# Epsilon, power and shift of two layer norms: from VectorE and GpSimd to GpSimd alone, between its softmax divisions

## The chip, the core and the metric

The kernel runs on one core of a Trainium2 chip. The core has a matrix engine (TensorE, PE in the profile; its weight loads are shown as PEld), a vector engine (VectorE, DVE), an activation engine (ScalarE, ACT), a general engine (GpSimd, POOL) and a sync engine that only issues transfers here (SyncE, SP). Each runs its own list of instructions in the order in which they were written, and waits for the others by semaphores. The metric is the device time of one execution in microseconds; before the change the median of three runs is 1526.4 us (1526.15 to 1528.2).

## The reference

One block of a cross-attention network in float32: 128 sequences of 128 tokens with 256 features, a context of the same size, 16 heads, a hidden layer of 1024. Cut to its core:

```python
q, k, v = heads(query @ Wq + bq), heads(key @ Wk + bk), heads(values @ Wv + bv)
scores = einsum('bhqd,bhkd->bhqk', q, k) / sqrt(16)
attn = softmax(where(j < i, scores, -1e30)); attn[:, :, 0, :] = 0
x = layer_norm(query + (attn @ v) @ Wo + bo, ln1_g, ln1_b)
ffn = relu(x @ W1 + b1) @ W2 + b2
out = layer_norm(x + ffn, ln2_g, ln2_b)

def layer_norm(x, g, b):
    mu = mean(x); var = mean((x - mu) ** 2)
    return (x - mu) * rsqrt(var + 1e-5) * g + b
```

## The kernel before, in words

The sequences are taken in 64 pairs, numbered p. A pair's tokens lie on 128 partitions, so that a tile of a pair has two columns of every per-token number. The work on a pair is spread over several steps of a software pipeline: step(p), which runs for p from 7 to 63, computes scores and softmax of pair p, the attention output and the first norm of pair p - 2, the first layer of the feed-forward part of pair p - 3, its second layer of pair p - 4, and the second norm of pair p - 5. In the steps from 7 to 62 the statistics of the two norms, two columns each, are made together in tiles of four columns; step 63 and the pairs at both ends make them apart.

The order of every engine is written out by hand: no scheduler moves an instruction. What is called first in step() stands first in the list of its engine.

The four-column tiles are mv (mean and variance of four token columns, made by both_stats: bn_stats and bn_aggr, L566 and L569), sd (first variance plus epsilon, L572 on VectorE; then, to the power of -0.5 in place, L1441 on GpSimd) and nb (minus mean times sd, L576 on VectorE, in both_shifts). ScalarE applies a norm as sd times x plus nb: L597 for the first norm (norm1), L634 for the second (norm2).

Around them stand, on GpSimd, the divisions of the softmax (sums, L440): the upper halves of the query rows come in two parts, heads 0 to 7 and heads 8 to 15, the lower halves in one part. In second_by_seven TensorE makes the second layer from seven products of eight matmuls each (L842), a Strassen-like scheme, that add up in three places of PSUM: px, py and pz. After a product, sum_of_seven (L878 on VectorE) adds the place's content to the residual t2; the next product onto the same place may start only when that has been read. In the order of the program: px, py, pz; sum 0 reads px; px again; sum 1 reads py; pz's second half; sum 2 reads px; py again; sums 3 and 4 read pz and py; px again; sum 5 reads px. Between the sums, second_by_seven calls what step() hands it for a given part: transposes of the next tokens (tokens, L250), of the weights that were divided (turn, L459), a reciprocal (L451), and, ahead of sum 5, both_shifts.

Behind that, hidden_by_seven makes the first layer from seven products too (L934, tiles phs); ScalarE and VectorE take part (L944, L947 to L962), and norm1 and norm2 run on ScalarE between them. On GpSimd follow add_bo (L257), residual1 (L609, L612) and finish (L640, L641, gain and bias of the second norm), and in the next step combine_hidden (tile hS, L827 to L830) and combine_normed (tile xS, L896 to L899), ahead of the next divisions.

Of the kernel before, what the change touches and what calls it, by code (L numbers as in the profile page):

```python
# [8 lines left out]
F32 = mybir.dt.float32  # L9
AF = mybir.ActivationFunctionType  # L10
ALU = mybir.AluOpType
AX = mybir.AxisListType

P = 128
NEG_INF = -1e30
LN_EPS = 1e-5
# [3 lines left out]
def tile_cross_attention_block(  # L20
# [22 lines left out]
    nc = tc.nc  # L43
# [19 lines left out]
    const = ctx.enter_context(tc.tile_pool(name="const", bufs=1))  # L63
# [73 lines left out]
    nc.sync.dma_start(c_first[:, 2:4], c[2:4].rearrange("b p d -> p b d"))  # L137
    power = const.tile([P, 4, 1], F32, tag="power", name="power")
    nc.gpsimd.memset(power, -0.5)
    ident = const.tile([P, P], F32, tag="ident", name="ident")  # L140
    make_identity(nc, ident)

# [111 lines left out]
    def add_bo(p):  # L254
        st = states[p]
        st["xb"] = proj.tile([P, 2, D], F32, tag="xb", name=f"xb_{p}")
        nc.gpsimd.tensor_tensor(  # L257
            st["xb"], tokens_of[p // 2][:, p % 2 * 2 : p % 2 * 2 + 2], bov_r[:, None, :].to_broadcast([P, 2, D]), ALU.add
        )
# [110 lines left out]
    def scores_both(p):  # L370

        st = states[p]
        for hi in range(2):
            st["sps", hi] = [
                at_bank(r if hi else (6, 7, 4, 5)[r], f"pss{hi}_{p}_{r}") for r in range(NS)
            ]
            room(p, hi)
        one, two = (0, 1), (2, 3)
        for strips, hi, m in (
            (two, 0, 0), (one, 1, 0), (two, 0, 1), (one, 1, 1),  # L380
            (two, 1, 0), (two, 1, 1), (one, 0, 0), (one, 0, 1),
        ):
            n = P if hi else HP
            for s in range(2):
                for r in strips:
                    strip, first = slice(32 * r, 32 * r + 32), s * P
                    nc.tensor.matmul(  # L387
                        st["sps", hi][r][
                            s * HP : (s + 1) * HP, m * 2 * n : (m + 1) * 2 * n
                        ].rearrange("p (e j) -> p e j", e=2),  # L390
                        st["qT"][strip, m, first + hi * HP : first + hi * HP + HP],
                        st["kT"][strip, m, :, first : first + n],
                        start=True, stop=True,
                    )
# [52 lines left out]
    def reciprocal(p, hi, part):  # L447
        st = states[p]
        rs = small.tile([P, H], F32, tag=f"rs{hi}", name=f"rs{hi}_{p}_{part.start}")
        rs = st["rs", hi, part.start] = rs[:, part]  # L450
        nc.vector.reciprocal(rs, st["su", hi][:, part])  # L451
# [44 lines left out]
    def weigh(p):  # L496

        st = states[p]
        pT = st.pop("pT")
        pc = at_bank(7, f"pc_{p}") if p > 1 else bank(f"pc_{p}")  # L500

        for m in range(KC):
            for s in range(2):
                at = (m * 2 + s) * P
                for j in range(NS):
                    nc.tensor.matmul(  # L506
                        pc[32 * j : 32 * j + 32, at : at + HP],
                        st["vd"][:, s, 4 * m + j].rearrange("p e d -> p (e d)"),
                        pT[:, 2 * s : 2 * s + 2, H + 2 * j + m, :],
                        start=True, stop=True,  # L510
                    )
            for s in range(2):
                at = (m * 2 + s) * P
                for e in range(2):
                    for j in range(NS):
                        nc.tensor.matmul(  # L516
                            pc[32 * j : 32 * j + 32, at + HP : at + P],
                            st["vz"][:, s, 4 * m + j, 2 * e : 2 * e + 2, :].rearrange(
                                "p e d -> p (e d)"
                            ),  # L520
                            pT[:, 2 * s : 2 * s + 2, 4 * j + 2 * m + e, :],
                            start=(e == 0), stop=(e == 1),
                        )
        st["pc"] = pc

    def context(p):
        pc = states[p].pop("pc").rearrange("p (u i) -> p u i", i=P)
        nc.scalar.copy(cxT.rearrange("p m s i -> p (m s) i")[:, :, 1:], pc[:, :, 1:])  # L528
# [29 lines left out]
    def both_stats(p):  # L558

        st, old = states[p - 2], states[p - 5]  # L560
        mv = small.tile([P, 4, 2], F32, tag="mv", name=f"mv_{p}")
        sd = small.tile([P, 4, 1], F32, tag="sd", name=f"sd_{p}")
        nb = small.tile([P, 4, 1], F32, tag="nb", name=f"nb_{p}")
        bs = small.tile([P, 4, 6], F32, tag="bsb", name=f"bsb_{p}")
        for u, t in enumerate((old["t2"][:, 0], old["t2"][:, 1], st["t1"][:, 0], st["t1"][:, 1])):
            nc.vector.bn_stats(bs[:, u], t)  # L566
        reciprocal(p, 1, TWO)
        for u in range(4):
            nc.vector.bn_aggr(mv[:, u], bs[:, u])  # L569
        for s, i, u in ((old, 2, 0), (st, 1, 2)):  # L570
            s["mv", i], s["sd", i], s["nb", i] = (v[:, u : u + 2] for v in (mv, sd, nb))
        nc.vector.tensor_scalar(sd, mv[:, :, 1:2], LN_EPS, None, ALU.add)  # L572
        return mv, sd, nb

    def both_shifts(mv, sd, nb):
        nc.vector.scalar_tensor_tensor(nb, mv[:, :, 0:1], -1.0, sd, ALU.mult, ALU.mult)  # L576

    def attention_sum(p):
        st = states[p]
# [213 lines left out]
    def low_maximum(p):  # L793
        st = states[p]
        nc.vector.tensor_reduce(st["nmx", 0], st["sm", 0], AX.X, ALU.max, negate=True)
# [581 lines left out]
    def step(p):  # L1377
        last = p == NP - 1
        weigh(p - 2)
        context(p - 2)  # L1380
        if p > 7:
            states[p - 4]["rest"].relu(1)
            states[p - 4]["rest"].relu(7)
            states[p - 4]["rest"].relu(3)
            states[p - 4]["rest"].relu(5)
        scores_both(p)
        if last:
            combine_hidden(p - 4, POOL_ALONE)
            add_bo(p - 1)
        else:  # L1390
            combine_hidden(p - 4, POOL_ALONE)
            combine_normed(p - 3)
        if not last:
            load_ahead(p)
        mask(p, 0, B)
        if last:
            mask(p, 0, A)
        mask_high(p, A)
        exponential_by_head(p, 1, ONES, True)
        mask_high(p, B)  # L1400
        exponential_by_head(p, 1, TWOS, True)
        if not last:
            mask(p, 0, A)
        low_maximum(p)
        if not last:
            exponential_by_head(p, 0, range(H), True)
            queries(p + 1)
        attention_out(p - 2)
        if not last:
            reciprocal(p, 1, ONE)  # L1410
        attention_sum(p - 2)
        if last:
            stats(p - 2, states[p - 2]["t1"], 1)
            deviation(p - 2, 1)
            shift(p - 2, 1)
            values(p)
            values_out(p)
            stats(p - 5, states[p - 5]["t2"], 2)
            deviation(p - 5, 2)
            norm1(p - 2)  # L1420
            exponential_by_head(p, 0, range(H), True)
            sums(p, 1, ONE)
            sums(p, 1, TWO)
            shift(p - 5, 2)
            turn_x1(p - 2)
            turn(p, 1, 0)
            second_by_seven(p - 4)
            residual1(p - 3)
            sums(p, 0, ALL)
            turn(p, 1, 1)  # L1430
            hidden(p - 3, range(FC))
            turn(p, 0, 0)
            bring(p, nc.sync, LATE_FIRST[: len(EVERY) // 2])
            return
        project_keys(p + 1)
        copy_keys(p + 1, (0,))
        values(p)
        joint = both_stats(p)
        sums(p, 1, ONE)
        sums(p, 1, TWO)  # L1440
        nc.gpsimd.tensor_tensor(joint[1], joint[1], power, ALU.pow)  # L1441
        ahead = p + 2 < NP
        second_by_seven(p - 4, {
            1: lambda: (tokens(p + 2, "x") if ahead else None, turn(p, 1, 0)),
            2: lambda: tokens(p + 2, "c") if ahead else None,
            3: lambda: (reciprocal(p, 0, ALL), turn(p, 1, 1)),
            5: lambda: both_shifts(*joint),
        })
        sums(p, 0, ALL)
        add_bo(p - 1)  # L1450
        residual1(p - 3)
        hidden_by_seven(p)
        finish(p - 5)
        store(p - 5)
        bring(p, nc.sync, LATE_FIRST)
# [56 lines left out]
    for s in range(2):  # L1512
# [8 lines left out]
        mv = small.tile([P, 2], F32, tag="mvl", name=f"mv_last_{s}")  # L1521
        nc.vector.bn_stats(bs, t2[:, s])
        nc.vector.bn_aggr(mv, bs)
        sd = small.tile([P, 1], F32, tag="sdl", name=f"sd_last_{s}")
# [39 lines left out]
```

## Time and profile before

| | |
|---|---|
| median of three runs | 1526.4 us |
| profiled execution, its own time | 1528.55 us |
| its span, first to last instruction | 1526.8 us |
| mean granted TensorE clock | 0.997 |
| share of the chain that ended last: TensorE | 92% |
| DVE, issue, ACT, POOL, DMA in that chain | 3%, 1%, 1%, 1%, 1% |
| L440, divisions on GpSimd | 192 of 1900 ns, 362.0 us |
| costliest lines of the chain | L934 23%, L842 pX 11%, py 7%, pz 7% |

The profile lists, per engine, how long it was busy, and for each line of the kernel the number of instructions, the mean time of one and what the engine had waited for. The chain is followed back from the last instruction, at each step to what released it; an engine with a large share of it sets the time. In a view by time a row gives start, duration, engine, line, operation and tiles, with x8 for eight such instructions in a row. Durations of neighbouring instructions of one engine overlap a little, since they are pipelined; the distance from start to start is the safer number.

### The profile page before, as it was taken

How to read it: one execution, taken by the hardware profiler on the slowest of the kernel's cores; microseconds unless marked ns; L12 is line 12 of the kernel's file. 1: busy time of each engine (PE TensorE's matmuls, PEld its weight loads, DVE VectorE, ACT ScalarE, POOL GpSimd, SP SyncE). 2: the span in 40 equal slices, each digit the busy share in tenths (PEclk: the TensorE clock that was granted, in tenths of full speed). 3: DMA queues.
4: the chain of work that ended last, by engine and by line, in shares of the span. 5: the costliest groups of instructions: out<-in, count | busy, mean ns of one | idle time of the engine just before them, and what ended most of it. 6: DMA issues, size and time to landing. Idle time of an engine off the chain costs nothing.

```text
span 1526.8 us, 53815 instructions
## 1 busy us (share of the span) xinstructions
PE 1500.5 (98%) x19270; PEld 1387.0 (91%) x19270; DVE 1368.1 (90%) x2835; ACT 1313.8 (86%) x5271; POOL 1258.1 (82%) x1118
## 2 busy tenths in 40 slices
PE   8999999999999999999999999999999999999888
PEld 6788999999999999999999999999999999999887
DVE  7989999999999999999999999999999999999844
ACT  5667999999999999999999999999989999999942
POOL 6878888888888888888888888888888888888862
PEclk9999999999999999999999999999999999999999
DMA  9356655655655565665556656566556556555431
GB/s 199 80 119 144 143 143 135 134 144 125 156 136 131 139 141 133 150 141 133 139 137 138 148 136 139 133 136 141 145 135 135 143 129 152 139 128 132 112 98 42
DMA packets 415318, 204.63 MB, mean 134 GB/s; under 512 B 282448, under 2 KB 383056, under 8 KB 415056
## 3 DMA queue, kind: packets, MB, share of 16 engines
q1 hardware_dynamic: 412768, 199.34, 56.3%
q8 instruction: 158, 2.59, 0.8%
q10 hardware_dynamic: 2288, 1.85, 0.5%
q14 instruction: 104, 0.85, 0.2%
HBM read 70.26 MB, written 33.29 MB: 68 GB/s over the span
## 4 chain that ended last, share of the span: by engine, by line
PE 92%; DVE 3%; ACT 1%; issue 1%; POOL 1%; DMA 1%; SPq 0%; POOLq 0%; DVEq 0%; ACTq 0%
PE phs L934 23%; PE pX L842 11%; PE pq L264 7%; PE py L842 7%; PE pz L842 7%; PE po L535 7%; PE pv L304 7%; PE pk L264 7%; PE pss L387 6%; PE pc L516 3%; PE ph L742 3%; PE pc L506 2%; ACT hT L750 1%; ACT sm L805 0%; PE py L762 0%
## 5 line engine op out<-in xcount | busy, mean ns | idle before, releaser
L440 POOL TENSOR_TENSOR sm<-sm,rs 128x1024 f32<-128x1024 f32 x192 | 362.0, 1900 | 24.8 <-DVE rs L451 18.8
L805 ACT ACTIVATE sm<-pss,nmx 128x128 f32<-128x128 f32 x944 | 328.5, 403 | 40.8 <-issue 36.3
L805 ACT ACTIVATE sm<-sm,nmx 128x64 f32<-128x64 f32 x944 | 313.7, 403 | 0.0
L805 ACT ACTIVATION_READ_ACCUMULATOR sm<-sm,nmx 128x1 f32 x912 | 234.0, 257 | 0.0
L459 DVE STREAM_TRANSPOSE tb<-sm 128x1024 f32<-128x1024 f32 x186 | 223.5, 1204 | 3.3 <-POOL sm L440 3.3
L805 ACT ACTIVATION_READ_ACCUMULATOR sm<-pss,nmx 128x1 f32 x912 | 221.9, 243 | 0.0
L965 ACT ACTIVATE hT<-hT,b1e_c 128x256 f32<-128x256 f32 x448 | 191.1, 499 | 19.2 <-DVE hT L956 19.1
L934 PE MATMUL phs<-xS,w1t 128*128 128x128 f32 x1344 | 159.2, 275 | 0.0
L934 PEld LDWEIGHTS phs<-xS,w1t 128*128 128x128 f32 x1344 | 154.6, 192 | 0.0
L788 DVE TENSOR_REDUCE nmx<-pss 128x4 f32<-128x512 f32 x236 | 151.0, 682 | 0.0
L640 POOL TENSOR_TENSOR t<-t,g_r 128x512 f32<-128x512 f32 x62 | 80.2, 1294 | 84.1 <-ACT t L634 83.9
L827 POOL TENSOR_TENSOR hS<-hT 128x512 f32<-128x512 f32 x57 | 72.3, 1268 | 87.5 <-ACT hT L965 86.4
L842 PE MATMUL pX<-wt,hS 128*128 128x128 f32 x960 | 131.9, 281 | 9.5 <-DVE t L878 5.5
L842 PEld LDWEIGHTS pX<-wt,hS 128*128 128x128 f32 x960 | 117.3, 193 | 18.7 <-issue 17.0
L294 ACT ACTIVATE kT<-pk,bkh,half 128x256 f32<-128x256 f32 x252 | 130.6, 588 | 4.0 <-PE pk L264 4.0
L264 PE MATMUL pq<-xT,wq 128*128 128x256 f32 x504 | 125.4, 392 | 0.0
L535 PE MATMUL po<-wo,cxT 128*128 128x256 f32 x512 | 121.3, 380 | 0.8 <-ACT cxT L528 0.8
L304 PE MATMUL pv<-wv,cT 128*128 128x256 f32 x512 | 121.0, 379 | 0.0
L264 PE MATMUL pk<-cT,wk 128*128 128x256 f32 x504 | 119.2, 379 | 0.0
L934 PE MATMUL phs<-x1T,w 128*128 128x128 f32 x896 | 118.3, 275 | 0.0
L401 DVE TENSOR_TENSOR sm<-pss,neg 128x256 f32<-128x256 f32 (+1 forms) x276 | 108.4, 436 | 6.0 <-PE pss L387 2.5
L535 PEld LDWEIGHTS po<-wo,cxT 128*128 128x128 f32 x512 | 96.9, 190 | 14.5 <-ACT cxT L528 1.3
(170 smaller groups left out, 4046.4 us busy)
## 6 DMA issues: line engine op xcount, KB each, us to landing
pT<-tb SPq DMA_DIRECT2D x976, 96.0 KB, 2.2
x1t<-tbx SPq DMA_DIRECT2D x252, 64.0 KB, 2.7
x1T<-x1t SPq DMA_DIRECT2D x63, 256.0 KB, 3.0
out_dram<-t SPq DMA_DIRECT2D x63, 256.0 KB, 3.2
xb<-in_x_dram SPq DMA_DIRECT2D x124, 128.0 KB, 4.1
cb<-in_ctx_dram SPq DMA_DIRECT2D x124, 128.0 KB, 3.8
x<-in_x_dram SPq DMA_DIRECT2D x31, 512.0 KB, 4.7
w<-in_L_xattn_W_dram SPq DMA_DIRECT2D x2, 1024.0 KB, 8.4
```

The source lines that it names most:

```text
L264: nc.tensor.matmul(ps[:, m * TP : (m + 1) * TP], w[:, k, m * P : (m + 1) * P], src[:, k, :], start=(k == 0), stop=(k == KC - 1),)
L294: nc.scalar.activation(st["kT"][:, m, e, :], pk[:, m * TP : (m + 1) * TP], AF.Identity, bias=bkh[:, m, e : e + 1], scale=half[:, e : e + 1],)
L304: nc.tensor.matmul(pv[:, s * D : (s + 1) * D], st["cT"][:, k, s * P : (s + 1) * P], wv[:, k, :], start=(k == 0), stop=(k == KC - 1),)
L401: nc.vector.tensor_tensor(st["sm", hi][:, 4 * r : 4 * r + 4, :], st["sps", hi][r][:, : 4 * n].rearrange("p (n j) -> p n j", j=n), no[:, No ...
L440: nc.gpsimd.tensor_tensor(sm[:, part, :], sm[:, part, :], rs[:, :, None].to_broadcast([P, part.stop - part.start, n]), ALU.mult,)
L459: nc.vector.transpose(st["tb"][:, :, at : at + 256].rearrange("p j (n a) -> p n j a", a=32), st["sm", hi].rearrange("p h j -> p (h j)")[:, ...
L535: nc.tensor.matmul(po[:, s * D : (s + 1) * D], cxT[:, k, s, :], wo[:, k, :], start=(k == 0), stop=(k == KC - 1),)
L788: nc.vector.tensor_reduce(st["nmx", 1][:, 4 * r : 4 * r + 4], st["sps", 1][r].rearrange("p (n j) -> p n j", j=P), AX.X, ALU.max, negate=True,)
L805: nc.scalar.activation(sm[:, h, :], src, AF.Exp, bias=nmx[:, h : h + 1], scale=1.0, **({"accum_out": st["su", hi][:, h : h + 1]} if summed ...
L842: nc.tensor.matmul(out, left(k), right(k), start=(first and k == 0), stop=(k == FC // 2 - 1), skip_group_check=True,)
L934: nc.tensor.matmul(ps[:, i * P : (i + 1) * P].rearrange("p (n a) -> p n a", a=32), left(i), right, start=(i == 0 and which not in self.ONT ...
L965: nc.scalar.activation(self.hT[:, f], self.hT[:, f], AF.Relu, bias=b1e_c[:, f : f + 1], scale=1.0,)
```

## The change

Two four-column constants are added (epsilon and minus one). The addition of epsilon leaves VectorE's both_stats. both_shifts becomes four tensor_tensor instructions on GpSimd (add epsilon, power, times mean, times minus one), and is called where the power stood before, behind the second of the three divisions; VectorE's call of it ahead of sum 5 goes.

```diff
     power = const.tile([P, 4, 1], F32, tag="power", name="power")
     nc.gpsimd.memset(power, -0.5)
+    eps = const.tile([P, 4, 1], F32, tag="eps", name="eps")
+    nc.gpsimd.memset(eps, LN_EPS)
+    minus = const.tile([P, 4, 1], F32, tag="minus", name="minus")
+    nc.gpsimd.memset(minus, -1.0)
...
-        nc.vector.tensor_scalar(sd, mv[:, :, 1:2], LN_EPS, None, ALU.add)
         return mv, sd, nb

     def both_shifts(mv, sd, nb):
-        nc.vector.scalar_tensor_tensor(nb, mv[:, :, 0:1], -1.0, sd, ALU.mult, ALU.mult)
+        nc.gpsimd.tensor_tensor(sd, mv[:, :, 1:2], eps, ALU.add)
+        nc.gpsimd.tensor_tensor(sd, sd, power, ALU.pow)
+        nc.gpsimd.tensor_tensor(nb, mv[:, :, 0:1], sd, ALU.mult)
+        nc.gpsimd.tensor_tensor(nb, nb, minus, ALU.mult)
...
         joint = both_stats(p)
         sums(p, 1, ONE)
         sums(p, 1, TWO)
-        nc.gpsimd.tensor_tensor(joint[1], joint[1], power, ALU.pow)
+        both_shifts(*joint)
         ahead = p + 2 < NP
         second_by_seven(p - 4, {
             1: lambda: (tokens(p + 2, "x") if ahead else None, turn(p, 1, 0)),
             2: lambda: tokens(p + 2, "c") if ahead else None,
             3: lambda: (reciprocal(p, 0, ALL), turn(p, 1, 1)),
-            5: lambda: both_shifts(*joint),
         })
```

On GpSimd, step 26 as an example, from the last of xS to the residual. Before (a name ends in the number of its buffer; rs_26_0 and rs_26_8 are reciprocals of pair 26):

```order
L899 TENSOR_TENSOR xS_9149<-x1T_9018,xS_9149 128x128
L440 TENSOR_TENSOR sm_9105<-sm_9105,rs_26_0_9219 128x1024
L440 TENSOR_TENSOR sm_9105<-sm_9105,rs_26_8_9244 128x1024
L1441 TENSOR_TENSOR sd_9237<-sd_9237,power 128x4
L440 TENSOR_TENSOR sm_9105<-sm_9105,rs_26_0_9310 128x1024
L257 TENSOR_TENSOR xb_9326<-x_8042,bov_r 128x512
```

The same place after the change, where line numbers are 4 to 6 higher:

```order
L905 TENSOR_TENSOR xS_9172<-x1T_9041,xS_9172 128x128
L444 TENSOR_TENSOR sm_9128<-sm_9128,rs_26_0_9242 128x1024
L444 TENSOR_TENSOR sm_9128<-sm_9128,rs_26_8_9267 128x1024
L579 TENSOR_TENSOR sd_9260<-mv_9259,eps 128x4
L580 TENSOR_TENSOR sd_9260<-sd_9260,power 128x4
L581 TENSOR_TENSOR nb_9261<-mv_9259,sd_9260 128x4
L582 TENSOR_TENSOR nb_9261<-nb_9261,minus 128x4
L444 TENSOR_TENSOR sm_9128<-sm_9128,rs_26_0_9335 128x1024
L261 TENSOR_TENSOR xb_9350<-x_8062,bov_r 128x512
```

Three instructions more stand between the second and the third division; nothing else moves on GpSimd.

On VectorE, the same step, from the statistics to the sum that reads py. Before:

```order
L569 BN_AGGR mv_9236<-bsb_9239 128x2 x4
L572 TENSOR_SCALAR sd_9237<-mv_9236 128x4
L878 TENSOR_TENSOR t_22_8957<-t_22_8957,pX_9256 128x128
L250 STREAM_TRANSPOSE xT_9288<-xb_8410 128x512
L459 STREAM_TRANSPOSE tb_9290<-sm_9105 128x8x4x32
L878 TENSOR_TENSOR t_22_8957<-t_22_8957,py_9257 128x128
```

After:

```order
L573 BN_AGGR mv_9259<-bsb_9262 128x2 x4
L884 TENSOR_TENSOR t_22_8980<-t_22_8980,pX_9281 128x128
L254 STREAM_TRANSPOSE xT_9313<-xb_8431 128x512
L463 STREAM_TRANSPOSE tb_9315<-sm_9128 128x8x4x32
L884 TENSOR_TENSOR t_22_8980<-t_22_8980,py_9282 128x128
```

The sum that reads px now follows the statistics directly; further on in the step, L576 ahead of the last L878 is gone too. Lists of the other engines are the same.

## The prediction

> **What bounds the kernel now.** I read the page's first part, then the instructions that the change touches, then one ordinary step of the steady loop in order of time on each engine (the columns there are start, duration, engine, line, operation, tiles, and in brackets the idle time before it and what ended it).
>
> ```profile
> PE 1500.5 (98%) x19270; PEld 1387.0 (91%) x19270; DVE 1368.1 (90%) x2835; ACT 1313.8 (86%) x5271; POOL 1258.1 (82%) x1118
> L572 DVE TENSOR_SCALAR sd<-mv x56: 282/1586/1818, 155.9 to 1425.1; 128x4 f32<-128x4 f32 x56
> L1441 POOL TENSOR_TENSOR sd<-sd,power x56: 1015/1019/1029, 158.6 to 1428.4; 128x4 f32<-128x4 f32 x56
> L576 DVE SCALAR_TENSOR_TENSOR nb<-mv,sd x56: 459/461/709, 162.0 to 1431.2; 128x4 f32<-128x4 f32 x56
> ```
>
> TensorE (PE) sets the time; what the change is worth is therefore what TensorE waits for in a step. A step lasts (1425.1 - 155.9) / 55 = **23.08 us**. The odd row is L572: adding epsilon to four columns takes 1586 ns on VectorE (DVE), though once it took 282. One ordinary step shows why. TensorE first:
>
> ```profile
> 546.84 1.05 PE L842 MATMUL pX<-w,hT 128*128 128x128 f32 x8
> 547.73 1.06 PE L842 MATMUL py<-wt,hS 128*128 128x128 f32 x8
> 548.62 1.06 PE L842 MATMUL pz<-w,hT 128*128 128x128 f32 x8
> 549.75 1.13 PE L842 MATMUL pX<-wt,hS 128*128 128x128 f32 x8
> 550.72 1.06 PE L842 MATMUL pz<-wt,hT 128*128 128x128 f32 x8
> 551.67 1.13 PE L842 MATMUL py<-w,hS 128*128 128x128 f32 x8
> 552.64 1.06 PE L842 MATMUL pX<-wt,hS 128*128 128x128 f32 x8
> 553.53 0.72 PE L934 MATMUL phs<-x1T,w 128*128 128x128 f32 x5
> ```
>
> These are the seven products of the second layer, eight matmuls each. From start to start an undisturbed one takes 0.89 us (546.84 to 547.73 to 548.62, and 552.64 to 553.53). The fourth product starts 1.13 after the third, that is 0.24 late; it then takes 0.97 instead of 0.89 (0.08 for starting again); the sixth starts 0.06 late and takes 0.08 too long. All seven take 553.53 - 546.84 = 6.69 instead of 7 x 0.8925 = 6.25: **0.44 us of TensorE are lost here in a step.** Now VectorE and GpSimd (POOL) beside it:
>
> ```profile
> 547.47 0.33 DVE L569 BATCH_NORM_AGGREGATE mv<-bsb 128x2 f32<-128x6 f32 x4
> 547.83 1.59 DVE L572 TENSOR_SCALAR sd<-mv 128x4 f32<-128x4 f32 x1
> 549.33 0.27 DVE L878 TENSOR_TENSOR t<-t,pX 128x128 f32<-128x128 f32 x1
> 550.16 1.20 DVE L459 STREAM_TRANSPOSE tb<-sm 128x1024 f32<-128x1024 f32 x1
> 551.28 0.24 DVE L878 TENSOR_TENSOR t<-t,py 128x128 f32<-128x128 f32 x1
> 552.08 0.24 DVE L878 TENSOR_TENSOR t<-t,pX 128x128 f32<-128x128 f32 x1
> ...
> 547.09 0.46 POOL L899 TENSOR_TENSOR xS<-x1T,xS 128x128 f32<-128x128 f32 x1
> 547.50 3.75 POOL L440 TENSOR_TENSOR sm<-sm,rs 128x1024 f32<-128x1024 f32 x2
> 551.21 1.02 POOL L1441 TENSOR_TENSOR sd<-sd,power 128x4 f32<-128x4 f32 x1
> 552.56 1.91 POOL L440 TENSOR_TENSOR sm<-sm,rs 128x1024 f32<-128x1024 f32 x1 [0.33 <-DVE rs L451]
> ```
>
> The fourth product adds onto pX, so it must wait until VectorE has read the first product out of it (L878 t<-t,pX, ends at 549.60; the product starts 0.15 later). The sixth waits in the same way for t<-t,py (ends 551.52, start 0.15 later). Both readers stand behind L572, and L572 ends at 549.42, where the first of GpSimd's two divisions ends (547.50 + 1.90 = 549.40). So the TENSOR_SCALAR does nothing for 1.3 us but wait for a GpSimd instruction to finish. One step of the 56 is a ready-made experiment, because GpSimd came 0.5 us later there:
>
> ```profile
> 1194.34 0.28 DVE L572 TENSOR_SCALAR sd<-mv 128x4 f32<-128x4 f32 x1
> 1196.49 1.25 DVE L459 STREAM_TRANSPOSE tb<-sm 128x1024 f32<-128x1024 f32 x1 [1.05 <-POOL sm L440]
> ...
> 1194.14 0.46 POOL L899 TENSOR_TENSOR xS<-x1T,xS 128x128 f32<-128x128 f32 x1
> ...
> 1195.14 1.06 PE L842 MATMUL pz<-w,hT 128*128 128x128 f32 x8
> 1196.03 1.06 PE L842 MATMUL pX<-wt,hS 128*128 128x128 f32 x8
> 1196.92 1.06 PE L842 MATMUL pz<-wt,hT 128*128 128x128 f32 x8
> 1198.05 1.13 PE L842 MATMUL py<-w,hS 128*128 128x128 f32 x8
> ```
>
> Here L572 waited only for the short L899 (both end at 1194.6) and the fourth product starts 0.89 after the third: **that wait is gone**. But the sixth now starts 0.24 late, since VectorE's transpose L459 waited for the late division. That is the wait that could take its place.
>
> **The change, part by part.**
>
> *L572 goes (56 times).* Without it VectorE, free at 547.80, reads pX as soon as the first product is out, at about 547.9 to 548.2; with the 0.15 seen above the fourth product could start at 548.35, and its undisturbed start is 546.84 + 3 x 0.8925 = 549.52. Cover: 1.2 us. Late next on VectorE is the transpose L459, which needs the first division, at 549.43 instead of 550.16. Everything after it moves 0.73 forward: t<-t,py ends at 550.79, so the sixth product could start at 550.94, against an undisturbed 546.84 + 5 x 0.8925 = 551.30. Cover: 0.36 us. t<-t,pX (552.08 now) ends at 551.6, the seventh product may start at 551.75, undisturbed 552.20: cover 0.44. All 0.44 us lost in a step go. In the first step L572 takes 0.9 and TensorE loses nothing; 55 steps remain: **55 x 0.44 = 24.2 us**.
>
> *L576 goes (56 x 0.46 on VectorE).* It lies ahead of VectorE's own wait for TensorE:
>
> ```profile
> 555.59 0.69 DVE L947 TENSOR_TENSOR hT<-hT,phs 128x512 f32<-128x512 f32 x1 [0.78 <-PE phs L934]
> 554.71 0.59 ACT L944 COPY hT<-phs 128x512 f32<-128x512 f32 x1 [0.94 <-PE phs L934]
> 557.39 1.09 ACT L597 ACTIVATE x<-t,nb,sd 128x256 f32<-128x256 f32 x2
> 559.55 1.29 POOL L640 TENSOR_TENSOR t<-t,g_r 128x512 f32<-128x512 f32 x1 [1.27 <-ACT t L634]
> ```
>
> VectorE idles 0.78 there; the 0.46 only lengthens that idle time. Worth 0. The same rows show the slack when TensorE is 0.44 us earlier: ScalarE (ACT) waits 0.94 for phs and keeps 0.50.
>
> *Three more four-column instructions on GpSimd a step.* The trace has no four-column add or multiply. Nearest rows:
>
> ```profile
> L1198 POOL TENSOR_TENSOR b1e_c<-b1e_c,b_c 128x8 f32<-128x8 f32 x1 | 0.2, 206 | 0.0
> POOL hS L827 <- ACT hT L965: 86.4, 56, 1.6
> POOL t L640 <- ACT t L634: 83.9, 59, 10.3
> POOL sm L440 <- DVE rs L451: 18.8, 55, 1.0
> ```
>
> An add of eight columns takes 206 ns: the lower end. The upper end is the power itself, 1019 ns for four. I take 0.2, since add and multiply are what that row is, and 0.08 before each for the result it reads (L898 ends at 547.01, L899, which reads it, starts at 547.09 in the step above): 3 x 0.28 = 0.84 us, queued between the second and the third division. The third division now waits 0.33 for its reciprocal, so it starts 0.5 later, at 553.1; behind it stand L257, L609, L612 and L640. L640 has 1.27 idle ahead of it, of which 0.44 go to the faster TensorE and 0.5 to this: 0.3 left, and another 1.54 (86.4 / 56) ahead of hS. Cost: **0**. The shift nb comes at about 553.1 instead of 554.5; its reader L597 starts at 557.39. Cost 0. At full price of the upper end the extra is 3.3 us a step, the rival below.
>
> [...]
>
> *Two memsets at the start, 0.1 each*, ahead of the identity that the warm-up reads: 0 to 0.2 us; I take 0.
>
> **Sum.** The profiled execution took 1528.55 us with a span of 1526.8; less 24.2 that is 1504.3. It lies 2.1 above the median of 1526.4; from the median: **1502.2 us**.
>
> **Rivals.**
>
> *The wait moves to the sixth product.* If the first division ended more than 0.36 us later against TensorE than now, the step would become that of 1194: 0.24 + 0.08 lost instead of 0.44, a gain of about 0.13 x 55 = 7 us, so 1519. For: that step exists, and the division follows a chain through a transfer (x1T) and eight GpSimd instructions (hS and xS, four each). Against: that chain starts from phs and is not touched by the change, and it was late in one step of 55; anything between 1502 and 1519 needs a delay between 0.36 and 0.8 in all steps. [...]
>
> *GpSimd becomes the bound (slower).* Its idle time in an ordinary step is 0.33 + 1.27 + 1.54 = 3.14 us. If each small instruction cost as much as the power (1.02 + 0.08, three times 3.3), GpSimd would work through without a pause and the step would be 23.08 + 0.16: 55 x 0.16 = 9 us slower, 1535. It decides at (3.14 / 3) - 0.08 = 0.97 us an instruction. For: the power takes 1.02 with the same four columns. Against: the 206 ns of L1198.
>
> *The waits of TensorE don't hang on L572*, and it stays at 1526: the step at 1194 speaks against it.
>
> **How the numbers follow.** Forecast 0.84 (1499 to 1506: 24.2 by the reading of starts, about 2, and a spread of the runs shown of 2); wait moved, whole or in part, 0.08; no change 0.03; GpSimd bound 0.05. The range of 8 in 10 is the forecast's own, stretched towards a partly moved wait: 1498 to 1511. Faster by over 0.2% (3 us, what a measurement of this kernel can tell): 0.84 + 0.08 = 0.92; same 0.03; slower 0.05.
>
> **What would show it.** Steps of 22.64 us; seven products in 6.25; no issue wait ahead of the fourth; the transpose L459 waiting for GpSimd by about 0.6; small adds and multiplies on GpSimd of 0.2; L640's idle time near 0.3. I would be wrong if the sixth product starts late in every step, if the small instructions take 0.6 or more, or if VectorE shows another long short-tile instruction.

## The result, and the profile after

The changed kernel takes **1504.9 us** (median of four runs, 1504.22 to 1505.53), against 1526.45 us before in the same comparison: a ratio of 0.9856, 95% interval 0.9839 to 0.9874, or 21.5 us. The forecast was 1502.2 us in a range of 1498 to 1511; its gain of 24.2 us corresponds to a ratio of 0.9841, inside the interval.

| | before | after |
|---|---|---|
| profiled execution, its own time | 1528.55 us | 1505.16 us |
| its span | 1526.8 us | 1503.4 us |
| busy: TensorE, VectorE, GpSimd | 1500.5, 1368.1, 1258.1 us | 1482.7, 1275.2, 1288.3 us |

From the page and from the views of the four-column tiles of the kernel after (behind the count: shortest, median and longest duration in ns, first and last start):

```profile
PE 1482.7 (99%) x19270; PEld 1380.9 (92%) x19270; DVE 1275.2 (85%) x2723; ACT 1312.1 (87%) x5271; POOL 1288.3 (86%) x1288
L579 POOL TENSOR_TENSOR sd<-mv,eps x56: 193/203/209, 158.1 to 1404.3; 128x4 f32<-128x4 f32 x56
L580 POOL TENSOR_TENSOR sd<-sd,power x56: 1017/1017/1023, 158.4 to 1404.6; 128x4 f32<-128x4 f32 x56
L581 POOL TENSOR_TENSOR nb<-mv,sd x56: 201/202/203, 159.5 to 1405.7; 128x4 f32<-128x4 f32 x56
```

VectorE is busy 93 us less and GpSimd 30 us more. Neither number is the gain; the gain is in TensorE's order of time. An ordinary step after the change, on TensorE, VectorE and GpSimd:

```profile
1105.68 1.05 PE L848 MATMUL pX<-w,hT 128*128 128x128 f32 x8
1106.57 1.06 PE L848 MATMUL py<-wt,hS 128*128 128x128 f32 x8
1107.47 1.06 PE L848 MATMUL pz<-w,hT 128*128 128x128 f32 x8
1108.36 1.06 PE L848 MATMUL pX<-wt,hS 128*128 128x128 f32 x8
1109.25 1.06 PE L848 MATMUL pz<-wt,hT 128*128 128x128 f32 x8
1110.15 1.06 PE L848 MATMUL py<-w,hS 128*128 128x128 f32 x8
1111.04 1.06 PE L848 MATMUL pX<-wt,hS 128*128 128x128 f32 x8
1111.93 1.06 PE L940 MATMUL phs<-x1T,w 128*128 128x128 f32 x8
...
1107.19 0.29 DVE L884 TENSOR_TENSOR t<-t,pX 128x128 f32<-128x128 f32 x1 [0.56 <-PE pX L848]
1108.27 1.25 DVE L463 STREAM_TRANSPOSE tb<-sm 128x1024 f32<-128x1024 f32 x1 [0.16 <-POOL sm L444]
1109.43 0.25 DVE L884 TENSOR_TENSOR t<-t,py 128x128 f32<-128x128 f32 x1
...
1106.33 3.75 POOL L444 TENSOR_TENSOR sm<-sm,rs 128x1024 f32<-128x1024 f32 x2
1110.04 0.20 POOL L579 TENSOR_TENSOR sd<-mv,eps 128x4 f32<-128x4 f32 x1
1111.85 1.90 POOL L444 TENSOR_TENSOR sm<-sm,rs 128x1024 f32<-128x1024 f32 x1
1117.94 1.29 POOL L646 TENSOR_TENSOR t<-t,g_r 128x512 f32<-128x512 f32 x1 [0.36 <-ACT t L640]
1122.15 1.27 POOL L833 TENSOR_TENSOR hS<-hT 128x512 f32<-128x512 f32 x1 [1.55 <-ACT hT L971]
```

The seven products follow one another at 0.89 us, 1111.93 - 1105.68 = 6.25 in all. The reader of px now waits for TensorE (0.56) and no longer the other way round. The step's length comes from two starts of the first product that lie 54 steps apart, after and before:

```profile
177.65 0.72 PE L848 MATMUL pX<-w,hT 128*128 128x128 f32 x5
1399.94 0.83 PE L848 MATMUL pX<-w,hT 128*128 128x128 f32 x6
```

```profile
177.54 1.05 PE L842 MATMUL pX<-w,hT 128*128 128x128 f32 x8
1423.99 1.05 PE L842 MATMUL pX<-w,hT 128*128 128x128 f32 x8
```

After: (1399.94 - 177.65) / 54 = **22.635 us**; before: 23.08. That is 24.2 us over 54 steps.

### The profile page after: what moved, and what is told of

Read it like the earlier page. It is cut to its first block, busy times and chain, and to the rows that moved or that the text cites. A ratio compares the mean times of both kernels' runs of the same rounds, so it can differ in the third digit from the quotient of the medians.

```text
span 1503.4 us, 53929 instructions
## 1 busy us (share of the span) xinstructions
PE 1482.7 (99%) x19270; PEld 1380.9 (92%) x19270; DVE 1275.2 (85%) x2723; ACT 1312.1 (87%) x5271; POOL 1288.3 (86%) x1288
## 4 chain that ended last, share of the span: by engine, by line
PE 93%; DVE 2%; ACT 2%; POOL 1%; DMA 1%; issue 1%; SPq 0%; ACTq 0%; POOLq 0%; DVEq 0%
PE phs L940 23%; PE pX L848 11%; PE pq L268 8%; PE pz L848 7%; PE py L848 7%; PE po L539 7%; PE pv L308 7%; PE pk L268 7%; PE pss L391 6%; PE pc L520 4%; PE ph L748 3%; PE pc L510 2%; ACT hT L756 1%; ACT sm L811 0%; PE py L768 0%
## 5 line engine op out<-in xcount | busy, mean ns | idle before, releaser
L463 DVE STREAM_TRANSPOSE tb<-sm 128x1024 f32<-128x1024 f32 x186 | 226.2, 1218 | 30.4 <-POOL sm L444 29.2
L848 PE MATMUL pX<-wt,hS 128*128 128x128 f32 x960 | 128.0, 277 | 4.4 <-DVE t L884 4.3
L646 POOL TENSOR_TENSOR t<-t,g_r 128x512 f32<-128x512 f32 x62 | 80.1, 1291 | 34.5 <-ACT t L640 34.4
```

The source lines that it names most:

```text
L463: nc.vector.transpose(st["tb"][:, :, at : at + 256].rearrange("p j (n a) -> p n j a", a=32), st["sm", hi].rearrange("p h j -> p (h j)")[:, ...
L848: nc.tensor.matmul(out, left(k), right(k), start=(first and k == 0), stop=(k == FC // 2 - 1), skip_group_check=True,)
```

## The experiments

Theory: the addition of epsilon on VectorE had to wait for the GpSimd instruction that was running, and what stood behind it in VectorE's list held TensorE up. Rivals: VectorE was relieved of work; sd and nb are ready earlier; GpSimd's new order matters.

**dummy_scalar: the wait alone.** To the kernel after, an instruction of the old form is added whose result nobody reads:

```diff
             s["mv", i], s["sd", i], s["nb", i] = (v[:, u : u + 2] for v in (mv, sd, nb))
+        spare = small.tile([P, 4, 1], F32, tag="spare", name=f"spare_{p}")
+        nc.vector.tensor_scalar(spare, mv[:, :, 1:2], LN_EPS, None, ALU.add)
         return mv, sd, nb
```

> The kernel after, with one TENSOR_SCALAR of four columns put back on VectorE where L572 stood; its result goes to a spare tile that nobody reads, and the arithmetic on GpSimd stays as it is after. Theory (the wait of this form for the running GpSimd division is what cost the time): it takes 1.59 us, ends with the first division, the fourth product starts 0.24 late, step 23.08, 1526 to 1529 us. Rival 1 (it was the early readiness of sd and nb, or the arithmetic that VectorE no longer does): nothing reads the spare tile and it is 0.28 us of work that fits in VectorE's idle time, so 1505. Rival 2 (the order of GpSimd's list): 1505 as well.

Measured: 1529.3 us in one run. The view of the spare tile in its profile:

```profile
L577 DVE TENSOR_SCALAR spare<-mv x56: 170/1576/1816, 155.9 to 1425.3; 128x4 f32<-128x4 f32 x56
```

The whole loss is back: the instruction takes 1576 ns again, and (1425.3 - 155.9) / 55 is 23.08. Since nothing depends on it and the arithmetic is that of after, readiness of sd and nb and the order on GpSimd are out as causes. The work itself costs at most the shortest of the 56, 170 ns. TensorE in a step:

```profile
1102.83 1.06 PE L850 MATMUL pz<-w,hT 128*128 128x128 f32 x8
1103.96 1.13 PE L850 MATMUL pX<-wt,hS 128*128 128x128 f32 x8
```

The fourth product starts 1.13 after the third again, 0.24 late. In the trace of before, L572 ends within 0.03 us of the end of a GpSimd instruction in all 56 steps, of a division in 55 of them.

**moved_only: another place, the same engine.** The kernel before, with the addition (and, in the text of the program, the power) called two instructions later:

```diff
-        nc.vector.tensor_scalar(sd, mv[:, :, 1:2], LN_EPS, None, ALU.add)
         return mv, sd, nb
+
+    def add_eps(mv, sd, nb):
+        nc.vector.tensor_scalar(sd, mv[:, :, 1:2], LN_EPS, None, ALU.add)
...
-        nc.gpsimd.tensor_tensor(joint[1], joint[1], power, ALU.pow)
...
-            1: lambda: (tokens(p + 2, "x") if ahead else None, turn(p, 1, 0)),
+            1: lambda: (tokens(p + 2, "x") if ahead else None, add_eps(*joint), to_power(*joint), turn(p, 1, 0)),
```

(to_power is the removed line as a function.)

> The kernel before, with nothing moved to GpSimd: VectorE still adds epsilon and makes nb, but the addition stands behind the sum that reads px and the transpose of the x tokens, right ahead of the transpose that needs the first division anyway. Theory (only the place in VectorE's list matters, since the instruction ends with the first division wherever it stands before that): the addition still ends with the division, seven products in 6.25, step 22.63, 1503 to 1506 us. Rival (VectorE has to be relieved of the work): VectorE is as busy as before, 1526.

Measured: **1504.5 us** (four runs, 1504.30 to 1504.99), ratio 0.9848, interval 0.9831 to 0.9864. VectorE and GpSimd in a step of its profile:

```profile
1107.34 0.29 DVE L883 TENSOR_TENSOR t<-t,pX 128x128 f32<-128x128 f32 x1 [0.21 <-PE pX L847]
1107.55 0.70 DVE L250 STREAM_TRANSPOSE xT<-xb 128x512 f32<-128x512 f32 x1
1108.17 0.58 DVE L575 TENSOR_SCALAR sd<-mv 128x4 f32<-128x4 f32 x1
1108.76 1.25 DVE L459 STREAM_TRANSPOSE tb<-sm 128x1024 f32<-128x1024 f32 x1
...
1106.83 3.75 POOL L440 TENSOR_TENSOR sm<-sm,rs 128x1024 f32<-128x1024 f32 x2
```

The addition still ends with the first division (1106.83 + 1.90 = 1108.73, against 1108.75), but in a place where the next instruction has to wait for that division too. The whole gain is there with no work moved to GpSimd. "VectorE had to be relieved" falls.

**shift_back: the other half.** The kernel after, with nb made by VectorE's one instruction ahead of sum 5, as before; the two multiplications on GpSimd go:

```diff
-        nc.gpsimd.tensor_tensor(nb, mv[:, :, 0:1], sd, ALU.mult)
-        nc.gpsimd.tensor_tensor(nb, nb, minus, ALU.mult)
...
+            5: lambda: vector_shift(*joint),
```

> The kernel after, with the shift nb back on VectorE as one SCALAR_TENSOR_TENSOR ahead of sum 5; epsilon and power stay on GpSimd. Theory (L576 was worth nothing, since VectorE idles behind it): same as after, 1503 to 1506 us, the instruction 0.4 to 0.6 us and ending with the third division, VectorE's wait for phs shorter by that. Rival (the gain comes from VectorE's busy time in general, 1586 ns of L572 and 461 of L576): a share of 461 / 2047 comes back, 21.5 x 0.225 = 5 us, so 1510.

Measured: 1506.6 us (1505.73 to 1508.29), ratio 0.9862, interval 0.9848 to 0.9877, which overlaps that of the whole change. In a step of its profile:

```profile
1113.28 0.69 DVE L583 SCALAR_TENSOR_TENSOR nb<-mv,sd 128x4 f32<-128x4 f32 x1
1114.49 0.69 DVE L954 TENSOR_TENSOR hT<-hT,phs 128x512 f32<-128x512 f32 x1 [0.19 <-PE phs L941]
...
1112.05 1.90 POOL L444 TENSOR_TENSOR sm<-sm,rs 128x1024 f32<-128x1024 f32 x1
```

The instruction ends with the third division (1113.97 against 1113.95) and VectorE's wait for phs is shorter for it (0.19, where the step of after has 0.80). The median lies 1.7 above that of after, where the rival had 5; between 0 and 2 us the medians don't tell. The steps do: the 55 from the first product at 155.25 to the one at 1400.60 take 1245.35 us, against 1244.93 after (155.01 to 1399.94).

**two_inputs and one_column: which forms wait.** Epsilon on VectorE at the old place, once as an instruction with two tiles as inputs, once as four instructions of one column (the addition on GpSimd goes in both):

```diff
+        nc.vector.tensor_tensor(sd, mv[:, :, 1:2], eps, ALU.add)
         return mv, sd, nb
```

```diff
+        for u in range(4):
+            nc.vector.tensor_scalar(sd[:, u], mv[:, u, 1:2], LN_EPS, None, ALU.add)
         return mv, sd, nb
```

> The kernel after, but epsilon is added on VectorE again, at the place of L572, as a TENSOR_TENSOR with two inputs in SBUF (variance and the constant tile) instead of a TENSOR_SCALAR. Theory A (what waits is every VectorE instruction that needs what GpSimd's running instruction holds, and the SCALAR_TENSOR_TENSOR L576, which ended with a GpSimd instruction in all its rows, has two SBUF inputs as well): it ends with the first division, about 1.6 us, 1526 to 1529 us. [...] Theory B (only the TENSOR_SCALAR form waits): 0.1 to 0.3 us, 1505.

> The kernel after, but epsilon is added on VectorE again, at the place of L572, as four TENSOR_SCALAR instructions of one column each. Theory A (the wait is by the form, whatever the size): the first ends with the first division; if GpSimd's second division takes over at once, the next ones wait up to 1.9 us more, so the fourth product starts 0.24 to 2.2 late: 1526 to 1640 us. Theory B (one column needs no second access and does not wait): four times 0.1 to 0.2 us, less than the 1.2 us of cover, 1505.

Measured: two_inputs 1529.0 us, one_column 1505.3 us, one run each. The rows of the addition in the one and the other:

```profile
L576 DVE TENSOR_TENSOR sd<-mv,eps x56: 1250/1581/1882, 156.1 to 1425.6; 128x4 f32<-128x4 f32 x56
```

```profile
L577 DVE TENSOR_SCALAR sd<-mv x224: 115/143/150, 156.4 to 1401.9; 128x1 f32<-128x1 f32 x112
```

And a step of one_column:

```profile
1107.43 0.30 DVE L577 TENSOR_SCALAR sd<-mv 128x1 f32<-128x1 f32 x4
...
1107.21 3.75 POOL L444 TENSOR_TENSOR sm<-sm,rs 128x1024 f32<-128x1024 f32 x2
```

Each of the two theories held in one run: A in two_inputs, B in one_column. With two inputs in SBUF the addition takes 1581 ns, as long as the old form did (1586); but the TENSOR_SCALAR of a single column never waits, 150 ns at most in 224 of them, although 218 of these began while a division was running. Four in a row last 0.30 us on VectorE and cost nothing at the end (1505.3 us). That a running GpSimd instruction holds something (theory A), or that one column needs no second access (theory B), no trace shows: both were the author's guesses. Why four columns in one instruction wait and one column does not, these runs don't show either.

**powers_1, powers_2, powers_3: how much GpSimd can take.** One, two or three more four-column powers a step behind the shift, into a spare tile:

```diff
         nc.gpsimd.tensor_tensor(nb, nb, minus, ALU.mult)
+        spare = small.tile([P, 4, 1], F32, tag="spare", name="spare")
+        for _ in range(2):
+            nc.gpsimd.tensor_tensor(spare, sd, power, ALU.pow)
```

> The kernel after, with one more four-column power on GpSimd a step behind the shift, its result in a spare tile that nobody reads: 1.02 + 0.08 us. GpSimd idles 0.36 ahead of L646 and 1.55 ahead of hS in a step after the change. Theory (that idle time is free): 1505, the idle times 0 and 0.8. Rival (each us on GpSimd reaches the end): 1505 + 56 x 1.1 = 1566.

> As powers_1 with two more powers a step: 2.2 us against 1.91 us of idle time. Theory (GpSimd becomes the bound there, the point from which the prediction's slower rival decides): no idle time on GpSimd, step 22.63 + 0.29, 1505 + 16 = 1521 us, 1515 to 1527. Rival (idle time elsewhere on GpSimd, or TensorE, still covers it): 1505.

> As powers_2 with three more powers a step. In powers_2 no idle time was left on GpSimd, the step was 22.71 and two powers took 2.06 us. Theory (GpSimd is the bound from there on): the third power comes on top in full, step 22.71 + 1.0 = 23.7, 1508 + 55 x 1.0 = 1563 us, slower than the kernel before. Rival (the 0.08 of powers_2 were TensorE's own, and GpSimd still has room): 1505 to 1515.

Measured: **1507.1, 1508.2 and 1568.1 us**, one run each. powers_1 had 2 us in two neighbouring steps: 23.24 and 24.03 from first product to first product, where nearly all others have 22.63. In the second of them:

```profile
1038.98 0.46 POOL L905 TENSOR_TENSOR xS<-x1T 128x128 f32<-128x128 f32 x1 [2.20 <-DMA x1T<-x1t]
1044.26 1.13 PE L851 MATMUL py<-w,hS 128*128 128x128 f32 x8 [1.16 <-DVE t L887]
```

GpSimd waited 2.20 us for the transfer of x1T, so its divisions came late, and TensorE's sixth product waited for the sum behind the transpose. That is the prediction's moved wait, in a single step; it accounts for 1.4 of the 2 us. Why the transfer came late, and the 0.6 in the step before, stay open. In powers_2 GpSimd, and in powers_3 TensorE:

```profile
1114.96 2.09 POOL L585 TENSOR_TENSOR spare<-sd,power 128x4 f32<-128x4 f32 x2
1117.02 1.91 POOL L444 TENSOR_TENSOR sm<-sm,rs 128x1024 f32<-128x1024 f32 x1
1122.73 1.28 POOL L649 TENSOR_TENSOR t<-t,g_r 128x512 f32<-128x512 f32 x1
1125.32 1.28 POOL L836 TENSOR_TENSOR hS<-hT 128x512 f32<-128x512 f32 x1
```

```profile
1107.61 1.06 PE L851 MATMUL pz<-wt,hT 128*128 128x128 f32 x8
1109.55 1.16 PE L851 MATMUL py<-w,hS 128*128 128x128 f32 x8 [0.88 <-DVE t L887]
```

In powers_2 no bracket is left on GpSimd: it works without a pause, and the step is its own 22.69 (1102.63 to 1125.32, from hS to hS), 0.06 over the 22.635 of after. I had expected 0.29: two powers that read nothing of each other take 2.06 and not 2.2, which is most of the difference. The third power then comes on top in full: the first products of two steps start at 1104.04 and 1127.83, 23.8 us apart, and the kernel is slower than before. So the prediction's slower rival is real, from some 2 us of further GpSimd work a step, and it shows up at the place of the other rival: TensorE's sixth product waits for the sum behind the transpose that waits for a late division.

**before_again: the spread of before.**

> The kernel before, once more. The profiled execution of before lay 2.1 us above the median, and the loss of 0.44 us a step was read from it. If the difference lies in the steps (in how many of them the TENSOR_SCALAR L572 meets a short GpSimd instruction instead of the first division, each such step being 0.13 us shorter), a run near 1526.3 has some 15 such steps where the first profile had one. If it lies outside the steps (start, end, transfers), the step is 23.08 in all but one or two again and the first or the last 100 us differ.

Measured: 1527.5 us, span 1525.7, the step 23.07 in nearly all steps and L572 never shorter than 1228 ns. Its span is 1.1 us shorter than that of the first profile, and 0.8 of this lies ahead of the steps: the first product of the first one starts at 154.09, against 154.91. So the steps make little of the difference between these two executions; what makes the whole spread of before (1526.2 to 1530.3 in all comparisons) was not settled.

**turn_late, moved_turn_late, both_late: the same fault once more.** The last step (pair 63) is written apart. In the kernel after, TensorE in it:

```profile
1423.63 1.99 PE L848 MATMUL pz<-w,hT 128*128 128x128 f32 x8 [2.50 <-ACT sm L811]
1429.47 2.05 PE L848 MATMUL pX<-wt,hS 128*128 128x128 f32 x8 [3.85 <-DVE t L884]
1431.31 1.91 PE L848 MATMUL pz<-wt,hT 128*128 128x128 f32 x8
```

The fourth product waits 3.85 us for VectorE's sum, which stands behind two transposes that wait for others. turn_late moves one of them, both_late both:

```diff
-            turn_x1(p - 2)
-            turn(p, 1, 0)
-            second_by_seven(p - 4)
+            second_by_seven(p - 4, {1: lambda: turn_x1(p - 2), 5: lambda: turn(p, 1, 0)})
```

(turn_late leaves turn_x1 where it was; moved_turn_late is turn_late on moved_only.)

> The kernel after, and in the last step alone (pair 63) the transpose that waits for the first division stands ahead of sum 5 instead of ahead of sum 0. In the trace of after, the fourth product of that step starts 4.95 us late, behind VectorE's sum that reads px, which stands behind that transpose; and three products behind the pause take 0.95, 0.81 and 0.47 too long. Theory (the same kind of place in VectorE's list, once): these 7.2 us go, less some 0.3 for sum 5, which now waits for the transpose: 1498 us, 1497 to 1501. Rival (the last pair's weights come later by the move, and TensorE waits for them instead): 1505.

> moved_only (arithmetic of before, the addition of epsilon at another place on VectorE) with the move of turn_late. Theory: 1504.5 less the same 7 us, 1497 to 1500; the same as turn_late within 1 us, since the arithmetic's engine does not matter.

> turn_late, and in the last step the transpose of the normed tokens (L712) too stands behind sum 0, ahead of sum 1. In turn_late the fourth product still starts 2.35 us late, since sum 0 stood behind that transpose, which waited 1.46 for ScalarE's norm; and the four products behind the pause run at a granted clock of 0.54, 2.9 us too long. Theory: the fourth product starts 0 to 0.3 late, the sixth up to 0.5 late behind the transpose; if the clock stays up because the pause is short, 1502 less 2 to 5 us, 1497 to 1500; if the 2.5 us pause ahead of the third product alone brings the clock down, the slow stretch stays and the gain is 2 us, 1500. Rival (another wait takes over at once, at the fifth or sixth product, because ScalarE's norm is what ends the pause in any order): 1502.

Measured: turn_late 1501.9 us (ratio 0.9821, 0.9807 to 0.9834), moved_turn_late 1502.8 (0.9832, 0.9818 to 0.9845), both_late **1498.4 us** (1496.66 to 1500.52; ratio 0.9806, 0.9792 to 0.9819). These medians come from other comparisons than that of after; the traces compare the last step itself. From its first product to the first matmul of L748 it takes 16.09 us after, 14.14 in turn_late and 10.61 in both_late. So turn_late brought less than half of the 7 us expected, because sum 0 still stood behind the other transpose, and moved_turn_late missed its 1497 to 1500 too. TensorE in turn_late, then in both_late:

```profile
1427.21 2.04 PE L848 MATMUL pX<-wt,hS 128*128 128x128 f32 x8 [2.09 <-DVE t L884]
```

```profile
1421.58 2.08 PE L848 MATMUL pz<-w,hT 128*128 128x128 f32 x8 [2.51 <-ACT sm L811]
1423.44 1.76 PE L848 MATMUL pX<-wt,hS 128*128 128x128 f32 x8
1425.05 1.06 PE L848 MATMUL pz<-wt,hT 128*128 128x128 f32 x8
```

With both out of the way the fourth product follows the third without a pause. The pause of 2.51 us ahead of the third product stays, and behind it the third and fourth take 1.86 and 1.61 from start to start instead of 0.89. both_late is faster than the kernels before and after.

## Why the prediction was right, point by point

- *What bounds the kernel, and the 0.44 us a step*: right. Seven products take 6.25, the step went from 23.08 to 22.635, and 54 steps give 24.2.
- *L572 goes, cause and price*: right, and shown by adding the wait back alone (dummy_scalar, 1529.3) and by moving it (moved_only, 1504.5). What TensorE saw of the 1.59 us was 0.44 a step, as in the sum.
- *The sum*: 24.2 forecast, 21.5 by the medians. The two profiled executions differ by 23.4 (1528.55 to 1505.16). Of the 0.8 missing there, 0.7 lie in the last step. From the fourth product to the seventh TensorE takes 4.91 there after the change and 4.21 before (1429.47 to 1434.38, and 1453.85 to 1458.06): its stretch at a granted clock of 0.50, which the last section shows, lasted longer (10.2 us against 6.8, of them 4.5 and 3.1 from the fourth product's start on). The rest is the spread of the runs: the loss was read from an execution 2.1 above the median of its kernel. The term that was too large is the last one, the carrying over of a profile's difference to the median. How much too large is open: in the four later comparisons the kernel before had medians of 1527.8 to 1528.7 and not 1526.45, and the changed kernel was not run in them.
- *L576 worth 0*: right in the steps, where shift_back loses 0.4 us in 55; its median is not as sharp (0 to 2 us).
- *GpSimd's instructions*: 0.20 us each, as taken from the eight-column row; L646's idle time 0.36, against 0.3 forecast. Cost 0: right.
- *What I had not seen*: the reciprocal ahead of the third division now waits for ScalarE's last exponential (31.0 us in all, 0.55 a step). It cost nothing, since GpSimd was in the small instructions then.
- *Rivals*: the moved wait did not come in the kernel after. The transpose waited 29.2 us in all, 0.52 a step, close to the 0.6 that the prediction had counted in, and the sixth product started on time. GpSimd as the bound came when it was given 2 us more, not at the change's own 0.84.

## What to carry to other kernels

Here a VectorE instruction of four columns that took 1586 ns (the same form 170 at its shortest, in dummy_scalar), and ended within 0.03 us of the end of a GpSimd instruction, was a wait that the profile booked as work. Where a very small instruction takes that long, look at shortest and median duration together, and at what stands behind it in the engine's list. Before moving such work to another engine, try moving it behind whatever has to wait for the same event anyway (moved_only, 1504.5 us), or give it a form that did not wait (one_column, 1505.3). The cover of the engine that takes the work can be counted from its idle times; that count held here to some 0.2 us a step (powers_2).

## What the runs showed of the hardware

- At the place of L572 a TENSOR_SCALAR of four columns, though it reads a single tile in SBUF, lasted until the running GpSimd instruction ended (before: median 1586 ns, its end within 0.03 us of the end of one in all 56). A TENSOR_TENSOR of four columns with two inputs in SBUF took as long there (two_inputs: 1581), and L576, a SCALAR_TENSOR_TENSOR with two, ended within 0.02 us of the end of a division in all 56 (before: 461). A TENSOR_SCALAR of one column did not wait (one_column: 143, 150 at most).
- Around a pause in the last step TensorE's granted clock halved: to 0.50 for 6.8 us in before and 10.2 in after. For turn_late some 6.8 us can be estimated from mean clocks of 0.87 (1424 to 1427) and 0.54 (1427 to 1433.6), for both_late some 3.3 from the start of the slow third product (1421.58) and a mean clock of 0.85 (1424 to 1427). The kernel after, in stretches of the last step (length; busy us and count of PE, PEld, DVE, ACT, POOL; granted clock; share of the DMA engines; GB/s):

```profile
1414.00:1424.00 10.00, 7.50 (x106) 6.62 (x99) 9.61 (x22) 8.44 (x41) 7.70 (x8) 0.99 0.57 150
1424.00:1429.40 5.40, 1.62 (x8) 1.33 (x7) 2.56 (x8) 5.36 (x28) 5.13 (x7) 0.50 0.63 149
1429.40:1434.40 5.00, 4.93 (x25) 4.96 (x26) 0.83 (x3) 1.70 (x11) 3.31 (x5) 0.54 0.44 110
1434.40:1440.00 5.60, 5.60 (x32) 5.05 (x31) 3.22 (x5) 1.68 (x4) 3.13 (x2) 1.00 0.04 12
```

The clock is 0.50 to 0.54 up to 1434.4 and 1.00 from there on; the three products behind the pause of 3.85 us take 1.84, 1.71 and 1.36 instead of 0.89, some 2 us more in all. That pause did not bring the clock down by itself: the third product, behind a pause of 2.50 and ahead of the longer one, already takes 1.99 (1.06 in an ordinary step). Nor did a pause of this length always do it: in before and turn_late the third product takes 1.16 behind 2.51, and the clock went down in the next pause, of 4.68 and 2.09 us. In after and both_late it went down behind a pause of 2.5. What decides between them, these runs don't show.
